# Cross-attention and FP4 feed-forward: part of the first tiles' preparation moved to GpSimd, two small loads packed into another, correlation blocks ordered earlier

## The chip, the cores and the metric

The kernel runs on one core of a Trainium2 chip. The core has five engines that run beside each other, each with its own queue of instructions: TensorE (PE, matrix products), VectorE (DVE), ScalarE (ACT), GpSimd (POOL) and SyncE (SP, which here only issues transfers). The metric is the device time of one execution in microseconds (us); lower is better.

## The reference

Inputs are `x` and a context, both 64 x 128 x 256 in float32. With learned weights the reference computes two residual steps:

```python
# 1. correlation attention; q from layernorm(x), k and v from the context
q  = (layernorm(x) @ Wq + bq).transpose(0, 2, 1)      # 16 channels, length 128
k_ = (ctx @ Wq + bq).transpose(0, 2, 1);  v = the same as k_
corr = real(ifft(fft(q) * conj(fft(k_)))).mean(axis=(0, 1))      # 128 shifts
W, I = top_k(corr, 12);  W = softmax(W)
R3   = sum over the 12 of  W * roll(v, -I)
x = x + (R3 broadcast to 16 heads) @ Wout + bout
# 2. feed-forward with both operands of every product rounded to FP4
def fp4(t):            # blocks of 16 along the last axis
    scale = max|block| / 6
    return nearest of {0, .5, 1, 1.5, 2, 3, 4, 6} * sign * scale
n = layernorm(x)
h = silu(fp4(n) @ fp4(w_gate).T) * (fp4(n) @ fp4(w_up).T)        # 704 wide
x = x + fp4(h) @ fp4(w_down).T
```

The top 12 shifts depend on all of x and all of the context, so the attention term is known only when both have been read. It takes few distinct values: rows that share a residue are given the same 256 numbers, which the kernel keeps in four tiles `O[0]` to `O[3]` (128 x 256, and one more column that gives the mean of each row of O).

## The kernel before, in words

Only the part up to the first feed-forward tiles matters here, and what follows it in order.

**Loads and correlation (0 to about 55 us).** SyncE issues the loads in the order written in `LOADS`. Sixteen blocks `xt` of x, transposed, give the sums that the layernorm and the correlation need. Eight blocks `c0` to `c7` of the context follow (the last in two halves, `c7a`, `c7b`). For each block TensorE forms `pk` = Wq times the block (line L1077), ScalarE adds the bias `Bq` and writes `kT` (L1091), and TensorE adds the correlation of the block to `pg` (L1100, two matmuls a row of blocks). `Wq` (128 x 64 floats) and `Bq` (128 x 1) have loads of their own (L817, L818). Gate and up weights come as `Wg` in three loads (L827). VectorE and ScalarE quantise the weights meanwhile. The quantised weights become `WgL`, `WgH`, `WdH`, `WdL` by transposing transfers (L721); the operand of `WdH` is written by a cast on ScalarE (L754) from `Wdn`, that of `WdL` on VectorE (L761 and L768).

**Attention (55 to about 68 us).** The correlation is copied to `Wcor` (L1150); VectorE finds the top 12 (two rounds of MAX8), softmax weights follow, and `Vn`, `Va`, `Wp` and `O` are formed on TensorE, ScalarE and VectorE (L1459, L1500, L1547, L1584, L1590). ScalarE needs another function table for square roots (a table load, L1549) and later one for Silu (L1621).

**The x stage.** There are 64 tiles of 128 rows. Loads of x bring four tiles at a time (`load_x`, L335): group q holds tiles 4q to 4q+3. `x_parts` (from L425) prepares a group, or a part of it:
- `neg` = minus the new mean of each row (L460, VectorE);
- X += O. On VectorE for the first groups (`add`, L446), for q > 2 by an accumulating transfer that GpSimd issues (L482);
- `cc` = X centred: on VectorE in one instruction together with O for tiles 0 and 1 (L471), else on ScalarE (L498);
- sums of squares on ScalarE (`junk`, L508); absolute maxima per block of 16 on VectorE (`am`, L518); scales and reciprocals (L534 to L561, L572, L578); division by the scale (L585); rounding to the FP4 grid (`k`, L593 to L606, and L338); and `xhl`, the result in two halves of 16 bits (L614);
- `xT`, its transpose: for tiles 0 to 3 by TensorE (L630) with copies out (L636), else by a transposing transfer (L643).

**The feed-forward (`group_ops`, from L1194).** For a tile t: `gu` = gate and up (L1220, TensorE), `g` = silu (L1226, ScalarE), `h` (L1233, VectorE), maxima of h per block (L1243), reciprocals (L1257), division (L1272: GpSimd, but VectorE for tile 0 and the last two), rounding (L1300, L1316 on ScalarE, L338 on VectorE), `hl` (L1325), a transposing transfer, and `pd` = the down product (L1369, L1371). L1388 adds it to X and the result is stored. The reductions of h also read a small strip behind each h that holds the least scale ("least strips", three of them, written on ScalarE at L1601).

**What sets the order.** Every operation is handed to `op(engine, cost, function, r=, w=, dl=, after=...)`. The `Order` class then plans: it keeps a free time for each engine and goes through the ready operations by earliest start and due time (`dl`), with the costs that are written in nanoseconds by hand; `rel` is an earliest time, `after` a mere order, `chain` forces one operation right behind another. The planned order is written out, and each engine's queue is then strictly that order. Waits between engines are semaphores, so an instruction that waits holds up all behind it on its engine. The line that chains a reciprocal to the next tile's h is `if t - 1 in recips`; the line that picks how O is added is `"D" if q > 2 else "V"`.

Of the kernel before, what the change touches and what calls it, by code (L numbers as in the profile page):

```python
# [12 lines left out]
F32 = mybir.dt.float32  # L13
# [6 lines left out]
ALU = mybir.AluOpType  # L20
# [239 lines left out]
@with_exitstack  # L260
def xattn_ffn(ctx: ExitStack, tc: tile.TileContext, x, xt, cx, wq, bq, wo, bo, wgu, wd, out):
    nc = tc.nc
# [87 lines left out]
    RG = (0.0, 0.0, 0.0)  # L350
    TC = 46000.0
    VB = 0
    TF = 49000.0
# [5 lines left out]
    LA = 4000.0  # L359
    BEFORE = 16  # L360
    HOT2 = 70000.0
    ZV, CV, EV = (0, *range(62, 64)), range(61, 64), range(64)
# [10 lines left out]
    FIRST = ((0, 2, "V"),)  # L373
    LOADS = "wg0 x0 wq wg1 x1 wg2 x2 x3 x4 x5 x6 x7 x8 x9 x10 x11 x12 wd x13 x14 x15 bq c0 c1 c2 c3 c4 c5 c6 c7a c7b wo bo"
    TO = 51000.0
# [20 lines left out]
    xT_of = {}  # L396
    adds = {}

    def x_stage(*a, **kw):
        for _ in x_parts(*a, **kw):  # L400
            pass
# [22 lines left out]

    def x_parts(R, q, i0, nt, fast, due, alu, pe_x=False, root=False, both=None, off=0):  # L425
        g, hq = q % 4, q // 4
# [12 lines left out]

        eng = "V"  # L440
        pe = fast
# [24 lines left out]
        for i in tiles:  # L466
            if fast:
                op(
                    "V",
                    336,  # L470
                    lambda i=i: V.scalar_tensor_tensor(  # L471
                        T["cc"].t[:, i], Xq.t[:, i0 + i], T["neg"].t[:, i : i + 1], O[g][:, 0:D], ALU.add, ALU.add
                    ),
                    r=[(Xq, i0 + i), T["neg"], ("O", g)],
                    w=[(T["cc"], i)],
                )
        if alu == "D":
            for i in tiles:
                adds[4 * q + i] = op(
                    "G",  # L480
                    900,
                    lambda i=i: G.dma_start(Xq.t[:, i0 + i], O[g][:, 0:D], accum_op=ALU.add),  # L482
                    r=[("O", g)],
                    w=[(Xq, i0 + i)],
                    lat=LA,
                    port=False,
                )
                adds[4 * q + i].rel = 0.0
        else:
            step = 1 if nt == 1 else 2  # L490
            for lo in range(0, nt, step):
                add(lo, lo + step)
        for i in tiles:
            if not fast:
                op(
                    "A",
                    400,
                    lambda i=i: A.activation(  # L498
                        T["cc"].t[:, i], Xq.t[:, i0 + i], AF.Identity, bias=T["neg"].t[:, i : i + 1]
                    ),  # L500
                    r=[(Xq, i0 + i), T["neg"]],
                    w=[(T["cc"], i)],
                )
# [225 lines left out]
    def d_scales(pool, ring, loaded, dg):  # L729
        s1 = pool.tile([P, 1], F32, name="s1")  # L730
        for h in range(2):
            amax_op(NF, sd[:, h : h + 1], Wdn[:, h : h + 1], NB, ["Wd"], ["sd"])
        op("V", 110, lambda: V.tensor_scalar(sd, sd, 1.0 / 24.0, TINY / 4.0, ALU.mult, ALU.max), w=["sd"])
        op("V", 600, lambda: V.reciprocal(rd, sd), r=["sd"], w=["rd"])
        op("V", 150, lambda: V.tensor_reduce(s1, sd.rearrange("p r b -> p (r b)"), AX.X, ALU.max), r=["sd"], w=["s1"])
        op("V", 130, lambda: V.tensor_scalar(dg[:, 0], ident, s1, None, ALU.mult), r=["s1"], w=["dg"])
        pm_d = ring.new()
        op("PE", 430, lambda: PE.matmul(pm_d.t[:, 0:P], ones, dg[:, 0], start=True, stop=True), r=["dg"], w=[pm_d], dl=18000.0)
        op("V", 200, lambda: V.tensor_reduce(s1, pm_d.t[:, 0:P], AX.X, ALU.max), r=[pm_d], w=["s1"])
        op(  # L740
            "V",
            70,
            lambda: V.tensor_single_scalar(p2[:, 2:3].bitcast(I32), s1.bitcast(I32), 0x7F800000, ALU.bitwise_and),
            r=["s1"],
            w=["p2d"],
        )
# [7 lines left out]
        op("A", 1370, lambda: A.copy(HdN[:, :, 0:NF], Wdn), r=[("Wd", 0), ("Wd", 1)], w=["HD"])  # L754
        S.rel = 0.0

    HdN = XA.bitcast(F16)[:, 0 : 4 * NF].rearrange("p (h n) -> p h n", h=2)
# [28 lines left out]
    with ExitStack() as ph1:  # L786
# [8 lines left out]
        )  # L795
        Wg = wp.tile([P, 11, D], F32, name="Wg")
        Wq = wp.tile([P, 2, 32], F32, name="Wq")
# [18 lines left out]
        loads = {  # L816
            "wq": (180, ["Wq"], lambda: SP.dma_start(Wq, wq)),  # L817
            "bq": (60, ["Bq"], lambda: SP.dma_start(Bq, bq)),  # L818
            "wo": (750, ["Wo"], lambda: SP.dma_start(Wo[:, :, 0:D], wo)),
# [3 lines left out]
        for n, (a0, a1) in enumerate(gch):  # L823
            loads[f"wg{n}"] = (
                340 * (a1 - a0),
                [("Wg", n)],
                lambda a0=a0, a1=a1: SP.dma_start(Wg[:, a0:a1], wgu[:, a0:a1]),  # L827
            )
# [11 lines left out]
        for n in LOADS.split():  # L840
            cost, w, f = loads[n]
            prev = (op("SP", cost, f, w=w, lat=LL, dl=at + DLS, after=prev),)
            at += cost
        Wqc = wp.tile([P, 2, 32], F32, name="Wqc")
        pw = r_q.new()
# [221 lines left out]
        loaded = (load_x(0, dl=TD, after=(wgl,)),)  # L1067
        d_scales(wp, r_q, loaded, dg)
        for j, b0, b1 in [(j, 0, 2) for j in range(7)] + [(7, 0, 1), (7, 1, 2)]:
# [4 lines left out]
            def f_k(ct=ct, pk=pk, b0=b0, b1=b1, n=n):  # L1074
# [12 lines left out]
            op("PE", 30 + 4.2 * n, f_k, r=[(ct, b) for b in range(b0, b1)] + ["Wq"], w=[pk], dl=TK)  # L1087
            op(
                "A",
# [8 lines left out]
            def f_g(bs=range(2 * j + b0, 2 * j + b1)):  # L1098
# [95 lines left out]
    def group_ops(tiles):  # L1194
# [16 lines left out]
        for i, t in enumerate(tiles):  # L1211
# [498 lines left out]
```

## Time and profile before

| | |
|---|---|
| median of 3 runs | 438.52 us (437.1 to 439.69) |
| the profiled execution | 438.42 us, of which 436.5 us are the span |
| first gate/up matmul (tile 0) | 71.64 us |
| gate/up of tile 2, tile 4 | 81.44, 92.67 us |
| busy DVE, ACT, POOL from 70 to 80 us | 9.21, 9.84, 3.85 of 10 |
| PE busy from 200 to 400 us | 199.74 of 200 |
| granted TensorE clock | 0.996 |

Times in lines of the profile are microseconds from the start of the span unless marked ns. A line of a timeline gives start, duration, engine (an engine's name with q is its queue, where transfers are issued), source line, operation, output and inputs by the program's names without buffer numbers, shapes, and how many instructions were taken together. A bracket at its end gives the idle time of that engine just before, and what ended it. In a line of a group the numbers behind the bar are the busy time in all, the mean duration of one in ns, and the idle time in front of them with what ended most of it.

### The profile page before, as it was taken

The page shows a single profiled execution, that of the slowest core. Times are in us where ns is not written, and L with a number is a line of the kernel's source. Part 1 is how long each engine was busy: PE and PEld are TensorE (multiplying, and loading weights), DVE is VectorE, ACT ScalarE, POOL GpSimd, SP SyncE. Part 2 cuts the span into 40 slices and gives each one's busy share as a digit, 9 for nine tenths or more (in the row PEclk, how much of TensorE's full clock was granted, in tenths as well). Part 3 has the DMA queues.
Part 4 walks back from the last instruction along what each step waited for, and adds up shares of the span by engine and source line. Part 5 has one row for each costly group of instructions (what it writes and reads, how often), then busy time and mean ns, then how long its engine had stood idle before and what let it go on. Part 6 is the DMA issues. An engine that isn't in the chain of part 4 may idle for free.

```text
span 436.5 us, 7999 instructions
## 1 busy us (share of the span) xinstructions
PE 418.5 (96%) x2950; PEld 267.5 (61%) x2950; DVE 393.3 (90%) x853; ACT 285.3 (65%) x480; POOL 137.4 (31%) x122
## 2 busy tenths in 40 slices
PE   8999889889898999999999999999999999999996
PEld 8556565446555656566666666666665666566686
DVE  7989589989999999989999989999999999978872
ACT  3887548788596696467946794887579666464410
POOL 1000000444434264344544444454434222324100
PEclk9999999899999999999999999999999999999999
DMA  8999999553797498578757877687678615952362
GB/s 292 414 384 419 322 231 280 124 105 71 152 163 162 106 220 178 137 134 210 158 136 148 212 157 163 139 173 154 117 162 164 156 38 125 188 123 66 96 167 74
DMA packets 152535, 76.61 MB, mean 176 GB/s; under 512 B 134448, under 2 KB 142000, under 8 KB 152496
## 3 DMA queue, kind: packets, MB, share of 16 engines
q1 hardware_dynamic: 145008, 69.29, 60.9%
q0 software_dynamic: 7488, 6.82, 10.9%
q8 instruction: 23, 0.38, 0.4%
q14 instruction: 16, 0.13, 0.1%
HBM read 27.76 MB, written 8.39 MB: 83 GB/s over the span
## 4 chain that ended last, share of the span: by engine, by line
PE 66%; DVE 14%; ACT 9%; DMA 8%; issue 2%; SPq 1%; ACTq 0%
PE gu L1220 38%; PE pd L1369 14%; PE pd L1371 8%; DMA xt<-in_xt_dram 6%; DVE hs L1243 3%; DVE h L1233 2%; DVE hl L1325 2%; DMA ct<-in_cx_dram 2%; ACT junk L508 2%; ACT cc L498 2%; ACT g L1226 1%; DVE am L518 1%; PE pk L1077 1%; DVE hr L1257 1%; DVE cc L585 1%
## 5 line engine op out<-in xcount | busy, mean ns | idle before, releaser
L1220 PE MATMUL gu<-WgH,xT 128*128 128x512 f16 (+1 forms) x768 | 193.1, 363 | 6.0 <-ACT g L1226 2.6
L1220 PEld LDWEIGHTS <-xT 128*128 128x128 f16 x1152 | 112.7, 98 | 116.5 <-issue 6.7
L1272 POOL TENSOR_TENSOR h<-h,hr 128x704 f32<-128x704 f32 x61 | 92.7, 1519 | 195.6 <-DVE hr L1257 168.8
L1220 PE MATMUL gu<-WgL,xT 128*128 128x512 f16 (+1 forms) x384 | 107.9, 363 | 0.0
L1226 ACT ACTIVATE g<-gu,ug 128x704 f32<-128x704 f32 x64 | 53.7, 840 | 43.7 <-PE gu L1220 43.5
L1300 ACT ACTIVATE hk<-h,c_half 128x1408 int16<-128x1408 f32 (+1 forms) x34 | 47.4, 1395 | 37.3 <-POOL h L1272 34.5
L1243 DVE TENSOR_REDUCE hs<-h 128x44 f32<-128x792 f32 x64 | 66.7, 1041 | 2.1
L1233 DVE SCALAR_TENSOR_TENSOR h<-gu,uh,g 128x704 f32<-128x704 f32 x64 | 55.9, 873 | 5.2 <-ACT g L1226 3.4
L482 POOL DMA_DIRECT2D X<-O x36 | 31.9, 983 | 74.3 <-DMA X<-in_x_dram 74.3
L1316 ACT ACTIVATE hc<-hk,c_sub 128x1408 f16<-128x1408 int16 (+1 forms) x32 | 45.6, 1426 | 0.5
L1369 PE MATMUL pd<-WdH,hT 128*128 128x256 f16 x352 | 43.7, 273 | 1.3 <-DMA hT<-hl 1.3
L1369 PEld LDWEIGHTS <-hT 128*128 128x128 f16 x352 | 34.4, 98 | 9.5 <-DMA hT<-hl 1.7
L1325 DVE TENSOR_TENSOR hl<-hc,hsb 128x1408 f16<-128x1408 f16 (+1 forms) x34 | 28.6, 842 | 0.2
L1325 DVE TENSOR_TENSOR hl<-hc,hsl 128x1408 f16<-128x1408 f16 (+1 forms) x34 | 28.5, 840 | 0.0
L1257 DVE RECIPROCAL hr<-hs 128x44 f32<-128x44 f32 x64 | 26.7, 418 | 0.2
L508 ACT ACTIVATE junk<-cc 128x256 bf16<-128x256 f32 x64 | 26.0, 406 | 0.4 <-DVE cc L471 0.2
L1371 PE MATMUL pd<-WdL,hT 128*128 128x256 f16 x192 | 26.2, 273 | 0.0
L1286 ACT ACTIVATE hsb<-hs 128x176 bf16<-128x176 f32 (+1 forms) x34 | 11.4, 335 | 19.8 <-DVE hs L1243 19.8
L498 ACT ACTIVATE cc<-X,neg 128x256 f32<-128x256 f32 x46 | 22.4, 498 | 2.9 <-DVE neg L460 2.9
L929 ACT ACTIVATE xsq<-xt,shift 128x1024 f32<-128x1024 f32 x16 | 17.8, 1145 | 9.5 <-DVE shift L925 6.2
L585 DVE TENSOR_TENSOR cc<-cc,rz 128x256 f32<-128x256 f32 x64 | 23.3, 418 | 0.1
L338 DVE TENSOR_SCALAR hc<-hc 128x1408 int16<-128x1408 int16 (+1 forms) x34 | 16.9, 496 | 5.7 <-ACT hc L1316 5.3
(252 smaller groups left out, 569.4 us busy)
## 6 DMA issues: line engine op xcount, KB each, us to landing
xt<-in_xt_dram SPq DMA_DIRECT2D x16, 512.0 KB, 8.1
ct<-in_cx_dram SPq DMA_DIRECT2D x7, 1024.0 KB, 13.9
X<-in_x_dram SPq DMA_DIRECT2D x12, 512.0 KB, 4.5
out_dram<-X SPq DMA_DIRECT2D x23, 256.0 KB, 2.4
X<-O POOLq DMA_DIRECT2D x36, 128.0 KB, 2.9
XA<-in_x_dram SPq DMA_DIRECT2D x4, 512.0 KB, 5.4
XA<-O POOLq DMA_DIRECT2D x16, 128.0 KB, 2.7
out_dram<-XA SPq DMA_DIRECT2D x7, 256.0 KB, 2.0
```

The source lines that it names most:

```text
L482: lambda i=i: G.dma_start(Xq.t[:, i0 + i], O[g][:, 0:D], accum_op=ALU.add),
L508: lambda i=i: A.activation(T["junk"].t, T["cc"].t[:, i], AF.Square, accum_out=T["ssq"].t[:, off + i : off + i + 1]),
L1220: PE.matmul(pg.t[:, c0:c1], src[:, b], w[:, k, c0:c1], start=(m == 0), stop=(m == 5))
L1226: lambda pg=pg, g=g: A.activation(g.t, pg.t[:, 0:NF], AF.Silu, scale=ug),
L1233: lambda pg=pg, g=g, i=i: V.scalar_tensor_tensor(B["h"].t[:, i, 0:NF], pg.t[:, NF:NG], uh, g.t, ALU.mult, ALU.mult),
L1243: lambda i=i: V.tensor_reduce(B["s"].t[:, i], B["h"].t[:, i].rearrange("p (jj b e) -> p b jj e", b=NB, e=2), AX.XY, ALU.max, apply_absolut ...
L1272: lambda i=i, zv=zv: (V if zv else G).tensor_tensor(per_block(B["h"].t[:, i, 0:NF], NB), per_block(B["h"].t[:, i, 0:NF], NB), spread(B["r" ...
L1300: lambda: A.activation(sub("k"), sub("h")[:, :, 0:NF], AF.Identity, bias=c_half, scale=24.0),
L1316: lambda: A.activation(flat("c"), flat("k"), AF.Identity, bias=c_sub, scale=SUB),
L1325: lambda e=e, part=part: V.tensor_tensor(B["hl"].t[:, 0:nt, e].rearrange("p t (jj n) -> p t jj n", jj=JJ), sub("c").rearrange("p t (jj n) ...
L1369: PE.matmul(pd, hT.t[:, b], WdH[:, :, b], start=(b == 0), stop=False)
L1371: PE.matmul(pd, hT.t[:, b], WdL[:, :, b], start=False, stop=(b == 5))
```

## The change

1. *Loads.* `Wq` and `Bq` lose their own loads. On the host they are put in front of the gate weights, in 66 more columns (64 + 1 + 1 of padding) of the same array; the first weight load brings them, and two small VectorE copies take them out.
2. *Correlation.* The due time of a block's `pg` matmuls was the same for all blocks; now it is earlier by 2.6 us for each block before the last. The cast L754 is placed behind the last `kT` on ScalarE.
3. *Table loads.* The one for square roots is due 12 us earlier and no longer waits for the first O; the one for Silu is due 8 us later.
4. *The x stage.* Tiles 0 and 1: O is added by a GpSimd transfer (`A0 = "D"`), behind the centring that includes it. Tiles 2 and 3: O is added on GpSimd, tile by tile; the centring is the VectorE one with O in it (`C2E = "V"`). Tiles 4 to 7: both the add and the centring run on GpSimd (`A1 = "P"`, `C1 = "G"`). Tiles 8 to 11: the add runs on GpSimd (`Q2A = "P"`). From tile 12 on nothing is different in kind.
5. *Least strips.* They are written on GpSimd, after the first product of the attention that gives O[0].
6. *Feed-forward.* A reciprocal is chained to the next tile's h only from t = 6 on (`CHAIN = 6`).

The planned order comes out of these together. In the changed kernel's written order GpSimd's queue runs: the three strips; the two accumulating transfers of tiles 0 and 1; the add of one of tiles 2 and 3; two accumulating transfers for tiles 12 and 13; four adds and four centrings (tiles 4 to 7); four adds (tiles 8 to 11); two more transfers; the add of the other of tiles 2 and 3; and then transfers between the divisions of h. In VectorE's queue the maxima of tiles 4 to 7 stand, as before, ahead of the end of tiles 2 and 3 and ahead of the first h.

```diff
@@ x_parts
-        eng = "V"
+        eng = "G" if alu in ("P", "PC") else "V"
...
-            if fast:
-                op(
+            if fast or cce == "V":
+                ccs_of[q] = op(
                     "V",
                     336,
...
         for i in tiles:
-            if not fast:
+            if cce == "G":
+                ccs_of[q] = op(
+                    "G",
+                    GC,
+                    lambda i=i: G.tensor_scalar(
+                        T["cc"].t[:, i], Xq.t[:, i0 + i], T["neg"].t[:, i : i + 1], None, ALU.add
+                    ),
+                    r=[(Xq, i0 + i), T["neg"]],
+                    w=[(T["cc"], i)],
+                )
+            elif not fast and cce != "V":
                 op(
                     "A",
                     400,
...
-            "wq": (180, ["Wq"], lambda: SP.dma_start(Wq, wq)),
-            "bq": (60, ["Bq"], lambda: SP.dma_start(Bq, bq)),
...
+        op("V", 100, lambda: V.tensor_copy(Wq.rearrange("p k n -> p (k n)"), Wall[:, 0:64]), r=[("Wg", 0)], w=["Wq"], dl=0.0)
+        op("V", 70, lambda: V.tensor_copy(Bq, Wall[:, 64:65]), r=[("Wg", 0)], w=["Bq"], dl=1000.0)
...
-                dl=TC,
+                dl=TC - CP * (7 - j),
             )
             cool.append(pg_op)
+        hd_op.after.add(k_op)
...
-            if t - 1 in recips:
+            if t - 1 in recips and t >= CHAIN:
...
-    op("A", 1300, lambda: A.activation(warm, c_half, AF.Sqrt), w=["tbl"], dl=TO, after=[*quick, t1_op])
+    op("A", 1300, lambda: A.activation(warm, c_half, AF.Sqrt), w=["tbl"], dl=TO - 12000.0, after=[t1_op])
...
     for t in h_tiles:
         op(
-            "A",
-            350,
-            lambda t=t: A.activation(
-                t[:, :, NF : NF + 2 * NB], ones[:, 0 : 2 * NB].unsqueeze(1).broadcast_to([P, 2, 2 * NB]), AF.Copy, scale=htiny
+            "G",
+            500,
+            lambda t=t: G.tensor_scalar(
+                t[:, :, NF : NF + 2 * NB], ones[:, 0 : 2 * NB].unsqueeze(1).broadcast_to([P, 2, 2 * NB]), htiny, None, ALU.mult
             ),
-            r=[("O", 3)],
             w=["least"],
+            after=first,
+            dl=TG + 12000.0,
         )
...
-        x_stage(R4, 0, i, n, True, TG + i * STEP0, e, True, True)
-    x_stage(R4, 0, 2, 2, False, TG + 2 * STEP0, "V", True, True)
+        x_stage(R4, 0, i, n, True, TG + i * STEP0, A0, True, True)
+    x_stage(R4, 0, 2, 2, F2, TG + DUE2, A2, P2, True, cce=C2E)
...
-        x_stage(R4, 1, i, n, False, TG + DUE1 + d, "V", p, True)
-    op("A", 1300, lambda: A.activation(warm, c_half, AF.Silu), w=["tbl"], dl=TG)
+        x_stage(R4, 1, i, n, False, TG + DUE1 + d, A1, p, True, cce=C1)
+    op("A", 1300, lambda: A.activation(warm, c_half, AF.Silu), w=["tbl"], dl=TG + SILU)
...
-            parts.append((due, x_parts(R4, q, 0, 4, False, due, "D" if q > 2 else "V", both=both, off=4 * n)))
+            parts.append((due, x_parts(R4, q, 0, 4, False, due, "D" if q > DQ else Q2A, both=both, off=4 * n)))
```

The new constants are `CP = 2600.0`, `DQ = 2`, `CHAIN = 6`, `Q2A = "P"`, `A0 = "D"`, `A1 = "P"`, `A2 = "P"`, `C1 = "G"`, `C2E = "V"`, `F2 = False`, `P2 = True`, `DUE2 = 7200.0`, `SILU = 8000.0` and `GC = 450.0`.

More of the change, by code (lines that the diff above doesn't have):

```diff
@@ L260, in xattn_ffn @@
 @with_exitstack
-def xattn_ffn(ctx: ExitStack, tc: tile.TileContext, x, xt, cx, wq, bq, wo, bo, wgu, wd, out):
+def xattn_ffn(ctx: ExitStack, tc: tile.TileContext, x, xt, cx, wo, bo, wgu, wd, out):
     nc = tc.nc
@@ L351, in xattn_ffn @@
     TC = 46000.0
+    CP = 2600.0
     VB = 0
@@ L360, in xattn_ffn @@
     BEFORE = 16
+    DQ = 2
+    CHAIN = 6
+    Q2A = "P"
+    A0 = "D"
+    A1 = "P"
+    A2 = "P"
+    C1 = "G"
+    C2E = "V"
+    F2 = False
+    P2 = True
+    DUE2 = 7200.0
+    SILU = 8000.0
+    GC = 450.0
     HOT2 = 70000.0
@@ L373, in xattn_ffn @@
     FIRST = ((0, 2, "V"),)
-    LOADS = "wg0 x0 wq wg1 x1 wg2 x2 x3 x4 x5 x6 x7 x8 x9 x10 x11 x12 wd x13 x14 x15 bq c0 c1 c2 c3 c4 c5 c6 c7a c7b wo bo"
+    LOADS = "wg0 x0 wg1 x1 wg2 x2 x3 x4 x5 x6 x7 x8 x9 x10 x11 x12 wd x13 x14 x15 c0 c1 c2 c3 c4 c5 c6 c7a c7b wo bo"
     TO = 51000.0
@@ L397, in xattn_ffn @@
     adds = {}
+    ccs_of = {}
     def x_stage(*a, **kw):
@@ L423, in roots, with x_parts @@
         op("V", 75, lambda: V.scalar_tensor_tensor(t, v, TINY / 4.0 / -3.2, y, ALU.mult, ALU.mult), r=[bv, by], w=[bt])
-    def x_parts(R, q, i0, nt, fast, due, alu, pe_x=False, root=False, both=None, off=0):
+    def x_parts(R, q, i0, nt, fast, due, alu, pe_x=False, root=False, both=None, off=0, cce=None):
         g, hq = q % 4, q // 4
@@ L478, in x_parts @@
             for i in tiles:
-                adds[4 * q + i] = op(
+                adds[4 * q + i0 + i] = op(
                     "G",
@@ L487, in x_parts @@
                 )
-                adds[4 * q + i].rel = 0.0
+                adds[4 * q + i0 + i].rel = 0.0
         else:
-            step = 1 if nt == 1 else 2
+            step = 1 if nt == 1 or eng == "G" else 2
             for lo in range(0, nt, step):
@@ L753, in d_scales @@
         G.memset(LdN[:, :, NF : 6 * P], 0.0)
-        op("A", 1370, lambda: A.copy(HdN[:, :, 0:NF], Wdn), r=[("Wd", 0), ("Wd", 1)], w=["HD"])
+        hd_op = op("A", 1370, lambda: A.copy(HdN[:, :, 0:NF], Wdn), r=[("Wd", 0), ("Wd", 1)], w=["HD"])
         S.rel = 0.0
+        return hd_op
     HdN = XA.bitcast(F16)[:, 0 : 4 * NF].rearrange("p (h n) -> p h n", h=2)
@@ L795, in xattn_ffn @@
         )
-        Wg = wp.tile([P, 11, D], F32, name="Wg")
+        Wall = wp.tile([P, 11 * D + 66], F32, name="Wall")
+        Wg = Wall[:, 66:].rearrange("p (a n) -> p a n", a=11)
         Wq = wp.tile([P, 2, 32], F32, name="Wq")
@@ L826, in xattn_ffn @@
                 [("Wg", n)],
-                lambda a0=a0, a1=a1: SP.dma_start(Wg[:, a0:a1], wgu[:, a0:a1]),
+                lambda c0=66 * (n > 0) + a0 * D, c1=66 + a1 * D: SP.dma_start(Wall[:, c0:c1], wgu[:, c0:c1]),
             )
@@ L1067, in xattn_ffn @@
         loaded = (load_x(0, dl=TD, after=(wgl,)),)
-        d_scales(wp, r_q, loaded, dg)
+        hd_op = d_scales(wp, r_q, loaded, dg)
         for j, b0, b1 in [(j, 0, 2) for j in range(7)] + [(7, 0, 1), (7, 1, 2)]:
@@ L1087, in xattn_ffn @@
             op("PE", 30 + 4.2 * n, f_k, r=[(ct, b) for b in range(b0, b1)] + ["Wq"], w=[pk], dl=TK)
-            op(
+            k_op = op(
                 "A",
@@ L1683 @@
     wgu = np.concatenate([wg[_PERM_F], wu[_PERM_F]], 0)[:, _PERM_D]
-    wgu_l = c(wgu.reshape(11, P, D).transpose(1, 0, 2))
+    wgu_l = wgu.reshape(11, P, D).transpose(1, 0, 2).reshape(P, 11 * D)
+    wgu_l = c(np.concatenate([wq_l.reshape(P, 64), bq_l, np.zeros((P, 1), bq.dtype), wgu_l], 1))
     wd_l = c(wd[_PERM_D][:, _PERM_F].reshape(2, P, NF).transpose(1, 0, 2))
@@ L1690 @@
         "cx": cx_l,
-        "wq": wq_l,
-        "bq": bq_l,
         "wo": wo_l,
```

## The prediction

> **What bounds the kernel now.** I read the page's first part, then busy time by stage, then the timelines of single engines around the stage that the change rearranges, then the groups of instructions. TensorE is nearly always busy:
>
> ```profile
> PE 418.5 (96%) x2950; PEld 267.5 (61%) x2950; DVE 393.3 (90%) x853; ACT 285.3 (65%) x480; POOL 137.4 (31%) x122
> ```
>
> That average hides three stages. Until 52.3 us transfers lead: the loads of x and context land one behind another (context blocks every 2.46 us, and the projection of each starts 0.15 to 0.3 us after it). From 55 to about 140 us a chain through VectorE leads. From 140 us on it is TensorE. The busy time by stage shows the last two (columns: length, then PE, PEld, DVE, ACT, POOL busy, granted clock, DMA share, GB/s):
>
> ```profile
> 70.00:80.00 10.00, 9.08 (x56) 4.82 (x55) 9.21 (x28) 9.84 (x29) 3.85 (x5) 1.00 1.04 309
> ...
> 120.00:140.00 20.00, 18.32 (x109) 10.43 (x108) 19.55 (x41) 16.62 (x36) 8.89 (x8) 1.00 0.89 171
> 140.00:200.00 60.00, 58.95 (x382) 37.10 (x381) 56.84 (x118) 38.36 (x62) 23.84 (x21) 1.00 0.71 154
> ```
>
> From 70 to 140 us DVE has hardly a gap, while PE idles. From 140 on PE lacks 1 us in 60. So a delay of the first FFN tiles that VectorE does not make good by 140 us stays in the total. PE's first waits:
>
> ```profile
> 79.51 0.84 PE L630 MATMUL pd<-ident_h,xhl 128*128 128x128 f16 x8 [0.57 <-DVE xhl L614]
> 81.44 1.00 PE L1220 MATMUL gu<-WgH,xT 128*128 128x512 f16 x2 [1.08 <-ACT xT L636]
> ...
> 92.67 0.59 PE L1220 MATMUL gu<-WgH,xT 128*128 128x512 f16 x2 [1.14 <-DVE h L1233]
> ```
>
> The first gate/up matmul (tile 0) starts at 71.64; 81.44 is tile 2, 92.67 tile 4, which waits for VectorE's h of tile 2. VectorE on the way there:
>
> ```profile
> 74.53 1.22 DVE L518 TENSOR_REDUCE am<-cc 128x64 f32<-128x1024 f32 x1
> ...
> 80.56 1.89 DVE L446 TENSOR_TENSOR X<-X,O 128x512 f32<-128x512 f32 x3
> ...
> 90.08 0.34 DVE L338 TENSOR_SCALAR hc<-hc 128x704 int16<-128x704 int16 x1 [1.76 <-ACT hc L1316]
> ...
> 91.67 0.85 DVE L1233 SCALAR_TENSOR_TENSOR h<-gu,uh,g 128x704 f32<-128x704 f32 x1
> ```
>
> The reduction at 74.53 (absolute maxima of tiles 4 to 7) is the place to watch. Behind it in VectorE's queue stand the last steps of tiles 2 and 3 (L338, L578, L614), h of tiles 0 and 1, and the xhl of tiles 4 to 7. Now the two queues that the change ties to it, SyncE's and GpSimd's:
>
> ```profile
> 66.99 1.95 SPq L335 DMA_DIRECT2D X<-in_x_dram  x3
> ...
> 76.14 4.68 POOL L482 DMA_DIRECT2D X<-O  x5 [74.35 <-DMA X<-in_x_dram]
> ```
>
> The first of these three loads (tiles 12 to 15) takes 7.2 us to land, at 74.1. GpSimd, idle for 74 us, starts adding O by DMA at 76.14, 0.75 us after the second load landed (75.39). Five issues take 4.68, 0.94 each.
>
> **The change, part by part.** The sum is made against the profiled execution, 438.42 us (span 436.5 and 1.9 around it), practically the median 438.52.
>
> *Loads.* Two go: Wq (32 KB) and Bq (128 packets of 4 B). Wq landed at 6.11 and the next weights at 8.21, where x loads follow each other by 1.25; Bq lies in the gap from 31.04 (last x) to 34.42 (first context), 3.38 against the usual 2.46. The excess is 0.85 and 0.9. Bq's own landing came 0.83 behind x's, so some is start of a new stream: I take 0.4 and 0.6, together 1.0 (bounds 0, since they overlap others, and 1.75). SyncE's queue loses two issues (0.42, 0.64); the loads behind them wait for the transfers in front, not for their issue. The two new VectorE copies (128x64, 128x1) lie in its idle start; the longest they could cost is 0.5 there, and then the loads would still hide it. The Trainium skill, "DMA: Bandwidth & Descriptors", Anatomy of one DMA, puts about 2 us of fixed cost on each transfer. By that the two would give 4.0; the landings, which overlap, do not allow it.
>
> *End of the correlation.*
>
> ```profile
> 52.56 1.37 ACT L754 CAST XA<-Wdn 128x1408 f16<-128x1408 f32 x1
> ...
> 53.83 0.37 ACT L1091 ACTIVATE kT<-pk,Bq 128x128 f32<-128x128 f32 x1
> ```
>
> The last kT stood behind the cast, though its matmuls were done at 53.28; and all twelve pg matmuls of six blocks (1.60) ran from 53.21 on. With the cast behind it and the earlier blocks done early, the last copy starts 0.5 earlier; I take 0.6 in all (0.4 to 0.9). The cast then ends near 54, and its transposes are issued at 58.97 only.
>
> *Attention.* L761 (0.53) comes in front of the first MAX: +0.2. The Sqrt table load (1.28, then 0.20) moves from between the Va copies to before them: +0.4 for the first. Sum of the prologue: -1.0 -0.6 +0.2 +0.4 = -1.0, and the first gate/up a little more, -1.1, because on VectorE a shorter centring (0.44) takes the place of the add at 65.94 (0.69) ahead of them (bounds -0.3 and -1.9).
>
> *VectorE's adds and centrings.* Six adds L446 (0.63 to 0.69) leave, 3.9; two centrings L471 (0.44) come, 0.9. ScalarE loses six centrings L498 (0.50) and three strips L1601 (0.43); from 80 to 100 us it is busy 14.7 of 20, so this by itself is worth nothing. The strips need 0.2 to 0.5 each on GpSimd, which was idle then; their readers, the reductions of h, come ten us later.
>
> *GpSimd's queue.* This is the step that decides. In the changed order GpSimd runs: strips; two DMA adds (tiles 0, 1); an add (tile 2); **two DMA adds of tiles 12 and 13**; four adds and four centrings of tiles 4 to 7; then tiles 8 to 11 and the rest. The two DMA adds of tiles 12 and 13 wait for the 66.99 load, and tiles 4 to 7, whose data landed at 64.31, are queued behind this wait. The reduction that was at 74.53 now waits for the last of these centrings. Its time:
> - the load lands at 74.1 - 1.0, plus what the two new DMA adds for tiles 0 and 1 (around 64, 256 KB) take from the transfers. At the 309 GB/s of 70 to 80 us that is 0.8, read and write counted 1.7, or 0: so 73.1 to 74.8, taken 74.0;
> - wake-up 0.75 (low: 0.15, as the context's readers): 74.75;
> - two DMA issues at 0.94: 76.6 (low: 1.1, by the 0.54 between their starts);
> - four two-input adds of 128x256, from the only such group on GpSimd:
>
> ```profile
> L1272 POOL TENSOR_TENSOR h<-h,hr 128x704 f32<-128x704 f32 x61 | 92.7, 1519 | 195.6 <-DVE hr L1257 168.8
> ```
>
>   scaled by 256/704: 0.55 each, 2.2: 78.8 (low 1.9);
> - four one-input centrings, no row: between the 128x256 IOTA (0.34) and the add (0.55); 0.45 taken, 1.8: last centring at 80.6 (all low 77.6, all high 82.2).
>
> The Trainium skill, "GPSIMD Engine Reference", 3.1, has one-input loops at 1.03 to 1.8 cycles an element, an estimate of 0.22 to 0.38 us each, which would end them 0.3 to 0.9 earlier. The same section says "use DVE for elementwise" stays the rule, which speaks against the move; the runs will show it.
>
> VectorE would be free for the reduction at 74.5 - 1.1 - 1.4 (two adds of tiles 4 to 7) - 0.7 (tiles 2, 3) + 0.9 = 72.2. It starts at 80.6 + 0.2 = 80.8: idle of 8.6 us, and 6.3 later than before. ScalarE waits too, with squares of these tiles standing ahead of tile 2's quantisation and the Silu table load.
>
> *What then catches up.* By h of tile 2: the three adds at 80.56 are gone (-1.9), and the idle of 1.76 at 90.08 mostly closes, since ScalarE now works beside a later VectorE (-1.7). So h of tile 2 comes at 91.67 + 2.7 = 94.4, and tile 4's matmuls follow. From there VectorE has the same work, 0.2 to 0.3 less, up to 140 us. Result: 438.4 + 2.7 - 0.3 = 440.8. All savings (1.1 in front, 3.0 of VectorE's work) are already inside; they pay about half of the wait. Unchaining tiles 1 to 5 lets a reciprocal be split from h: no work, between 0 and one 0.42 either way.
>
> **Rivals.**
> 1. *The lag is absorbed.* After tile 4 PE still idles at 110.80 (1.28), 115.97 (0.59), 130.56 (1.58), 174.22 (0.97): 4.4 us. If half of this closes because VectorE's later queue is shifted less than PE, the end is 440.8 - 2.2 = 438.6. For it: some of these end on a transfer. Against: those transfers follow VectorE's xhl and hl.
> 2. *Not slower: GpSimd is done early.* Same place, one quantity, the last centring. It decides at 80.6 - 2.4 = 78.2: before that the total falls below 438.4. With the low ends (77.6) it is 437.8; with the load landing 2 us sooner, as would follow if the whole transfer queue drains faster, 435.8. The floor, no wait at all, is 438.4 - 1.1 - 3.0 = 434.3. For it: wide bounds on wake-up and centring. Against: the load is the eighth in a full queue.
> 3. *Worse.* The DMA adds of tiles 0 and 1 collide with the transposes and X loads (DMA share 1.06 there), GpSimd's adds run slower beside VectorE: last centring at 82.2 or later, 442.4 to 443.5.
> 4. *Loads hidden anyway:* the prologue gives nothing, and all shifts by 1.0: 441.8. It lies within the forecast's own range.
>
> **How the numbers follow.** Forecast (439.5 to 442) 0.42; rival 1 0.20; rival 2 0.25; rivals 3 and 4 0.13. About 0.5% (2.2 us) can be told from no change. Under 436.3 lies most of rival 2's lower part and a mixture with 1: 0.25. Over 440.7: more than half of the forecast's case, and 3 and 4: 0.46. Between: 0.29. The range 435.0 to 443.5 leaves out one in ten at each end.
>
> **What would show it.** Right: GpSimd idle before its DMA adds until about 75, VectorE idle 7 to 9 us in front of a reduction at about 81, released by GpSimd's centring; tile 2's first gate/up at 84 to 86, tile 4's near 95; first gate/up near 70.5; PE busy without gaps from 140 on. Wrong: a centring that ends before 78, or tile 4 earlier than 92.7; the first gate/up not before 71.6 would refute the loads' part. A much faster result needs tiles 4 to 7 to be centred before VectorE asks for them.

## The result, and the profile after

The changed kernel takes 447.59 us (median; 446.97 to 447.93), the kernel before 438.52: a ratio of 1.0231, 95% interval 1.0201 to 1.0261. The forecast was 440.8 with a range up to 443.5. The direction was right, the size was not: +9.1 us instead of +2.3. The profiled execution took 447.93 us, with a span of 445.9.

The first part of its page, with the granted clock from the second part:

```profile
PE 419.5 (94%) x2944; PEld 267.6 (60%) x2944; DVE 395.0 (89%) x851; ACT 283.3 (64%) x471; POOL 152.7 (34%) x141
...
PEclk9999999579899999999999999999999999999999
```

The busy times hardly moved, GpSimd's excepted (137.4 to 152.7); PE's share fell because the span grew. The two lowest digits of the clock, 5 and 7, cover 78 to 100 us. Busy time by stage (columns: length, then PE, PEld, DVE, ACT, POOL busy, granted clock, DMA share, GB/s):

```profile
70.00:80.00 10.00, 7.30 (x36) 3.44 (x36) 2.14 (x10) 1.57 (x6) 6.69 (x10) 1.00 0.94 300
80.00:90.00 10.00, 2.18 (x11) 1.19 (x12) 8.48 (x15) 7.75 (x17) 7.46 (x10) 0.51 0.28 41
90.00:100.00 10.00, 10.00 (x44) 5.06 (x43) 8.59 (x16) 7.48 (x19) 2.33 (x2) 0.81 0.42 93
120.00:140.00 20.00, 20.00 (x125) 12.26 (x124) 19.59 (x46) 17.36 (x35) 7.93 (x7) 0.97 0.62 137
140.00:200.00 60.00, 58.11 (x377) 36.53 (x376) 57.73 (x122) 38.89 (x63) 25.74 (x22) 1.00 0.77 157
```

VectorE, 9.21 of 10 us busy from 70 to 80 before, now has 2.14, and GpSimd has 6.69. The hole in PE follows from 80 to 90. GpSimd's timeline (start, length, engine, line, operation, count, idle time before and its releaser):

```profile
73.31 1.77 POOL L497 DMA_DIRECT2D X<-O  x2 [7.25 <-DMA X<-in_x_dram]
74.45 3.40 POOL L461 TENSOR_TENSOR X<-X,O 128x256 f32<-128x256 f32 x4
77.20 4.21 POOL L513 TENSOR_SCALAR cc<-X,neg 128x256 f32<-128x256 f32 x4
80.80 3.32 POOL L461 TENSOR_TENSOR X<-X,O 128x256 f32<-128x256 f32 x4
```

This is the queue that the prediction drew: a wait for the load of tiles 12 to 15, two DMA issues, four adds, four centrings, and the reduction on VectorE behind the last of them. VectorE's timeline goes on:

```profile
81.45 1.22 DVE L543 TENSOR_REDUCE am<-cc 128x64 f32<-128x1024 f32 x1 [9.30 <-POOL cc L513]
82.58 1.70 DVE L338 TENSOR_SCALAR k<-k 128x512 int16<-128x512 int16 x1
...
103.72 0.46 DVE L1353 TENSOR_TENSOR hl<-hc,hsb 128x704 f16<-128x704 f16 x1
104.10 1.85 DVE L1353 TENSOR_TENSOR hl<-hc,hsl 128x704 f16<-128x704 f16 x1
```

The first line was predicted (80.8, idle of 8.6). The second and the last are what the prediction lacked. The form of L338 at 82.58 takes 0.29 elsewhere in this trace, and here 1.70. The two L1353 have the same shape, one after the other: 0.46 and 1.85. The first long one begins while GpSimd does the four adds from 80.80 to 84.12 and ends 0.16 us after the last of them. The second begins while GpSimd does the division of h below, and ends 0.39 us after it:

```profile
103.89 1.67 POOL L1300 TENSOR_TENSOR h<-h,hr 128x704 f32<-128x704 f32 x1
```

PE, in the same stretch, waits twice:

```profile
84.81 1.16 PE L655 MATMUL pd<-ident_h,xhl 128*128 128x128 f16 x8 [7.16 <-DVE xhl L639]
...
88.97 1.01 PE L1248 MATMUL gu<-WgH,xT 128*128 128x512 f16 x2 [3.00 <-DVE h L1261]
```

**An account of the loss.** Follow VectorE from the moment that O of tile 0 is written to the end of xhl of tiles 8 to 11; the first gate/up matmul of tile 8, behind those, starts some 4 us later. I split that time into idle time, *stretch* (what an instruction took beyond the usual duration of its line and shape in the same trace, summed), and ordinary work. What one takes as the usual duration moves the stretch of a run by half a us or so; the rest of the account follows from the trace alone.

| us | before | after | difference |
|---|---|---|---|
| O of tile 0 starts | 63.51 | 61.76 | -1.75 |
| VectorE idle | 3.23 | 11.45 | +8.22 |
| VectorE stretched | 0.19 | 5.25 | +5.06 |
| ordinary work | 45.80 | 42.91 | -2.89 |
| xhl of tiles 8 to 11 done | 112.72 | 121.38 | +8.66 |
| gate/up of tile 8 | 116.56 | 125.52 | +8.96 |
| last matmul ends | 433.21 | 442.38 | +9.17 |

The lag at 121 us is the lag at the end. The prediction had the first, second and fourth rows within 1.5 us. It had no third row. Of that row about half (2.7) lies in instructions beside GpSimd's adds (L610 at 65.33, L338 at 82.58, L576 at 85.02) and half (2.7) beside divisions of h (L338 at 102.46 and 111.30, L1353 at 104.10). The experiments ask whether that reading of the trace holds.

### The profile page after: what moved, and what is told of

The parts are those of the page before. It is cut to its first block, busy times and chain, and to the rows that moved or that the text cites. A ratio compares the mean times of both kernels' runs of the same rounds, so it can differ in the third digit from the quotient of the medians.

```text
span 445.9 us, 7993 instructions
## 1 busy us (share of the span) xinstructions
PE 419.5 (94%) x2944; PEld 267.6 (60%) x2944; DVE 395.0 (89%) x851; ACT 283.3 (64%) x471; POOL 152.7 (34%) x141
## 4 chain that ended last, share of the span: by engine, by line
PE 73%; DMA 10%; DVE 7%; ACT 4%; POOL 2%; issue 2%; SPq 1%; ACTq 0%; POOLq 0%
PE gu L1248 45%; PE pd L1397 16%; PE pd L1399 9%; DMA xt<-in_xt_dram 5%; DMA ct<-in_cx_dram 2%; DMA X<-in_x_dram 1%; ACT g L1254 1%; DVE hl L1353 1%; DVE h L1261 1%; PE pk L1104 1%; POOL X L461 1%; ACT hk L1328 1%; DVE cc L610 1%; DMA xT<-xhl 1%; POOL cc L513 1%
## 5 line engine op out<-in xcount | busy, mean ns | idle before, releaser
L1248 PE MATMUL gu<-WgH,xT 128*128 128x512 f16 (+1 forms) x768 | 195.2, 365 | 10.3 <-DVE h L1261 5.7
L497 POOL DMA_DIRECT2D X<-O x38 | 35.1, 968 | 10.4 <-DMA X<-in_x_dram 7.2
L1353 DVE TENSOR_TENSOR hl<-hc,hsl 128x1408 f16<-128x1408 f16 (+1 forms) x34 | 29.9, 879 | 0.0
L1353 DVE TENSOR_TENSOR hl<-hc,hsb 128x1408 f16<-128x1408 f16 (+1 forms) x34 | 28.5, 839 | 0.2
L543 DVE TENSOR_REDUCE am<-cc 128x64 f32<-128x1024 f32 (+1 forms) x17 | 19.6, 1152 | 9.4 <-POOL cc L513 9.3
L624 ACT ACTIVATE k<-cc,c_half 128x1024 int16<-128x1024 f32 (+1 forms) x16 | 17.9, 1118 | 14.9 <-DVE cc L610 14.9
L338 DVE TENSOR_SCALAR hc<-hc 128x1408 int16<-128x1408 int16 (+1 forms) x34 | 18.4, 541 | 6.3 <-ACT hc L1344 6.2
L610 DVE TENSOR_TENSOR cc<-cc,rz 128x256 f32<-128x256 f32 x64 | 23.9, 427 | 0.1
```

The costliest lines, as they stand in the source:

```text
L610: (G if alu == "G" else V).tensor_tensor(per_block(T["cc"].t[:, i], XB), per_block(T["cc"].t[:, i], XB), spread(T["rz"].t[:, i], XB), ALU. ...
L1248: PE.matmul(pg.t[:, c0:c1], src[:, b], w[:, k, c0:c1], start=(m == 0), stop=(m == 5))
L1353: lambda e=e, part=part: V.tensor_tensor(B["hl"].t[:, 0:nt, e].rearrange("p t (jj n) -> p t jj n", jj=JJ), sub("c").rearrange("p t (jj n) ...
```

## The experiments

Theories: **W**, the wait of the reduction behind GpSimd's queue; **S**, VectorE's instructions are held while GpSimd computes; **C**, the lower TensorE clock after the hole; **D**, the dropped chaining of h's reciprocals (`CHAIN = 6` lets the tiles below 6 run without it). The expectations were written before the letters were settled: in them theory A is W, and theory D is S, with the chaining as one of its cases. All ratios are to the kernel before, with 95% intervals.

**e1_order: tiles 4 to 7 go ahead of the DMA adds of tiles 12 and up.**

```diff
+    for t in adds:
+        if t >= 12:
+            adds[t].after.add(ccs_of[1])
     heat_buf(Q["pd"].new(), HOT2)
```

> The changed kernel, but the accumulating transfers of tiles 12 and up stand behind the four centrings of tiles 4 to 7 in GpSimd's queue; same instructions. Theory A (the wait for the load of tiles 12 to 15 in that queue costs the time): GpSimd's adds start when O[1] is there, about 68.1; with the steps of the changed kernel's own profile (0.69 an add, 0.9 to 1.0 a centring) and one add of tile 8 between, the last centring ends near 75.6, the reduction of tiles 4 to 7 starts near 75.8 instead of 81.45, VectorE's idle falls from 9.3 to 3 or 4 us, and the total falls by 5.5 to 8, to 439.5 to 442. Rival B (GpSimd is too slow for this work wherever it stands, or its adds slow VectorE down): idle above 6 us, total above 445.

Measured: 442.84 us, 1.0096 [1.0062, 1.0130], so 4.75 us of 9.1 come back (1.35% of 2.31% by the ratios, which compare each run with the kernel before of its own session). The total is just above the range of theory A. GpSimd, then VectorE:

```profile
68.08 4.12 POOL L461 TENSOR_TENSOR X<-X,O 128x256 f32<-128x256 f32 x5 [2.02 <-ACT O L1612]
72.57 3.69 POOL L513 TENSOR_SCALAR cc<-X,neg 128x256 f32<-128x256 f32 x4 [0.37 <-DVE neg L475]
```

```profile
76.30 1.22 DVE L543 TENSOR_REDUCE am<-cc 128x64 f32<-128x1024 f32 x1 [2.26 <-POOL cc L513]
```

The reduction comes 5.15 us sooner, and the idle time in the account falls from 11.45 to 4.88. The stretch rises from 5.25 to 7.38, since VectorE now works while GpSimd does tiles 4 to 11. W is half of the loss or a little more, and the time is still above the kernel before.

**e2_q1_back, e7_q2_vec, e8_q12_chain: GpSimd's arithmetic is taken back step by step.** e2 gives tiles 4 to 7 back to VectorE and ScalarE, e7 tiles 8 to 11 as well, e8 restores the chaining too.

```diff
-    A1 = "P"
+    A1 = "V"
-    C1 = "G"
+    C1 = None
...
-    Q2A = "P"
+    Q2A = "V"
...
-    CHAIN = 6
+    CHAIN = 0
```

> The changed kernel with tiles 4 to 7 prepared as before: O added on VectorE, centred on ScalarE. All else stays, the transfers for tiles 12 and 13 with their wait too, but nothing of VectorE's next work stands behind them. A: VectorE's idle before the reduction is under 1 us, the total 435.5 to 438 (prologue 1.3 us earlier than before, no adds for tiles 8 to 11 on VectorE). B' (the loss lies in other parts: transfers for tiles 0 and 1, unchained reciprocals, table loads): above 442.

> The run with tiles 4 to 7 prepared as before, and now the adds of tiles 8 to 11 on VectorE again too. CHAIN = 6 stays, and so do the additions on GpSimd for tiles 2 and 3. Theory D: at 74.8 to 79.8 three VectorE instructions were stretched from 0.93 to 3.99 us together while GpSimd added; without these adds that goes, two adds of 0.69 come to VectorE. Net 1.7 us less: 441.5 to 443. Rival (GpSimd's adds relieve VectorE): 444.5 to 446.

> As the last, and CHAIN = 0: of the x stage only tiles 0 to 3 remain changed (transfers for 0 and 1, GpSimd adds for 2 and 3, VectorE's centring for 2 and 3), with the strips, table loads, packed loads and correlation order of the change. Theories A and D together: no wait on GpSimd's queue in VectorE's, one stretched instruction (0.6 us at 65.3); total 436.5 to 439, as the kernel before. Rival (one of these remaining parts costs several us too): above 440.

Measured: e2 444.11, 1.0123 [1.0091, 1.0155], a miss of 6 us (the rival B' held); e7 440.52, 1.0075 [1.0052, 1.0097], 1 us below its range; e8 437.08, 1.0001 [0.9975, 1.0027]. In e2 the long wait is gone (idle 4.60), and yet it is slower than before: the stretch is 7.60. GpSimd, then VectorE beside it, in e2:

```profile
75.42 3.74 POOL L461 TENSOR_TENSOR X<-X,O 128x256 f32<-128x256 f32 x4
```

```profile
76.66 1.92 DVE L603 TENSOR_TENSOR slo<-am,shb 128x64 f16<-128x64 f32 x1
78.50 1.30 DVE L639 TENSOR_TENSOR xhl<-k,shb 128x512 f16<-128x512 f16 x1
```

The same two in e7, where GpSimd does not add these tiles:

```profile
76.09 0.37 DVE L603 TENSOR_TENSOR slo<-am,shb 128x64 f16<-128x64 f32 x1
76.39 0.41 DVE L639 TENSOR_TENSOR xhl<-k,shb 128x512 f16<-128x512 f16 x1
```

1.92 becomes 0.37, 1.30 becomes 0.41, although VectorE now adds O to four tiles more. That is S. Of what e7 still has stretched (4.77), 3.7 stands beside divisions of h:

```profile
92.76 1.51 POOL L1300 TENSOR_TENSOR h<-h,hr 128x704 f32<-128x704 f32 x1 [1.97 <-DVE hr L1285]
```

```profile
92.78 1.52 DVE L426 TENSOR_SCALAR y<-ssq 128x4 int32<-128x4 int32 x1
```

A 128x4 instruction (0.16 as a rule) lasts as long as GpSimd's. In the kernel before the chaining keeps this apart: beside the divisions of its trace run 61 instructions of h, 58 reductions of h and one other, none longer than usual by more than about 0.10. e8 restores it: stretch 1.04, time that of the kernel before. How much of this step is the stretch isn't shown: VectorE's idle time rises from 1.15 to 3.33, so xhl of tiles 8 to 11 is done only 0.6 us sooner (112.21 against 112.81). On PE three tiles of down products stand ahead of the gate/up of tile 8 in e7, four in e8, and that gate/up starts at 117.02 and 117.10; a tile of down products takes 1.85.

Undone in this order the parts are worth 1.1% (tiles 4 to 7), 0.5% (tiles 8 to 11) and 0.7% (chaining), that is about 4.7, 2.1 and 3.3 us, each with an uncertainty of 1 to 2. All others together are left with 0.0%, which can be gains and costs that cancel (f3 below has gains).

**e6_chain and e10_order_chain: the chaining alone, in the changed kernel and in e1.**

```diff
-    CHAIN = 6
+    CHAIN = 0
```

> The changed kernel with the reciprocal, the next h and its reduction chained for all tiles again (CHAIN = 0), nothing else. Theory D (while GpSimd runs a division of h, VectorE's short and fast-mode instructions last until it ends; the chain kept h and its reduction beside the division, and without it others land there: L338 at 102.46 took 0.93 for 0.35, L1353 at 104.10 took 1.85 for 0.52, L338 at 111.30 took 1.27 for 0.52): these stretches, 2.7 us, go, and with them part of the 2.5 us in which TensorE waited at 114; total 444.5 to 446.5. Rival: the order of the reciprocals is worth nothing next to the wait at 72 to 81: 447 to 448.

> The run with GpSimd's queue reordered (442.84), and CHAIN = 0. Theory D: the stretches at 98 to 107 us (2.4 us in three instructions) go, as in the step from 440.52 to 437.08: 439.5 to 441.5. Rival (as with the chain alone restored in the changed kernel, 448.4: VectorE's later xhl of tiles 8 to 11 then holds up tile 8): 442.5 to 444.

Measured: e6 448.40, 1.0251 [1.0210, 1.0292]; e10 443.36, 1.0145 [1.0109, 1.0181]. Both miss what theory D expected: no gain from what is worth 3.3 in e8. In e10 VectorE did gain: the stretch falls from 7.38 to 4.91, and xhl of tiles 8 to 11 is done at 113.81 instead of 116.69. But PE's timeline shows

```profile
118.43 1.04 PE L1248 MATMUL gu<-WgH,xT 128*128 128x512 f16 x2 [7.31 <-DMA xT<-xhl]
```

The restored chaining also changes the planned order on PE: only two tiles of down products stand ahead of the gate/up of tile 8, four in the kernel before, the changed one and e8. PE runs dry. The gate/up of tile 8 starts 2.4 earlier than in e1 (118.43 against 120.84), but two tiles of down products, 1.85 each, that e1 has behind it by then are still to do, and the last matmul ends at 438.43 (438.10). e6 has the same two tiles, and an idle time of 6.55 in the same place. So what the chaining is worth depends on this order, and 3.3 us is the price of the step from e7 to e8 only.

**e5_warm: 30 idle products in PE's queue keep the clock up** (their result is never read).

```diff
+    for _ in range(30 if q == 0 and i0 == 2 and i == 0 else 0):
+        PE.matmul(pt.t[:, 0:P], ident, ident, start=True, stop=True)
```

> The changed kernel with 30 idle products of 128x128 in TensorE's queue between gate/up of tile 1 and the transposes of tile 2, some 6.6 us of work where it waited 7.2; the output is the same. Theory C (part of the loss is that TensorE's granted clock falls to a half while it waits, 0.50 from 84 to 92 us): gate/up of tiles 2 and 3, 10.3 us in the changed kernel, takes 8 to 9 us, and the total falls by 1 to 2.5, to 445 to 446.5. Rival: VectorE sets the pace there whatever the clock: 447.2 to 448.

Measured: 447.69, 1.0215 [1.0174, 1.0255], against 447.59 for the changed kernel: the rival's range. The granted clock from 80 to 84 us (the figure before the last two), in the changed kernel and in e5:

```profile
80.00:84.00 4.00, 0.00 (x0) 0.00 (x0) 2.55 (x2) 3.94 (x13) 4.00 (x7) 0.52 0.00 0
```

```profile
80.00:84.00 4.00, 4.00 (x38) 4.00 (x37) 2.59 (x2) 3.94 (x13) 4.00 (x7) 1.00 0.00 0
```

The gate/up of tile 2 still starts at 88.94 (88.97), released by VectorE's h. In e5 the clock is higher from 88 to 96 us too (0.62 and 0.95, against 0.50 and 0.77). C is out: the low clock of an engine that waits for another cost nothing here.

**f1_dose: e3 (below) plus 24 GpSimd adds of 128x128 that nobody reads.** The rest of the queues is e3's.

```diff
+    for _ in range(24):
+        op("G", 10, lambda: G.tensor_tensor(dose, O[0][:, 0:P], O[0][:, 0:P], ALU.add), r=[("O", 0)], w=["dose"], after=first, port=False, dl=TG)
```

> The run with only the loads and correlation order changed, with 24 extra GpSimd additions of 128x128 into a tile that nothing reads, from the moment O[0] is written (about 62 us); the queues of the other engines are the same instruction for instruction, and nobody waits for the additions. Theory D (VectorE's instructions with two SBUF inputs or in a fast mode stand still while GpSimd computes): of some 0.4 us each they last to about 72 us, and 10 or more VectorE instructions there stretch by 0.2 to 0.5 each; reductions, reciprocals and instructions with an input in PSUM keep their times; total up by 2 to 5, to 439.5 to 442.5. Rival (only waits in queues cost): 437 to 438.

Measured: 437.61, 1.0006 [0.9983, 1.0028], e3 being at 0.9983. The total lies in the rival's range, so theory D missed the size. The adds ran from 62.05 to 75.9, and VectorE beside them was stretched, but by little: 1.99 in the account against 0.19, e.g. L611 with 0.96 where e3 has 0.76. Of that, 1.25 was taken out of VectorE's idle time (3.97 to 2.72). The GpSimd adds came 0.58 apart here, which may be why a held instruction soon got through; those of the changed kernel came 0.69 apart and the divisions took 1.52. This run says that the mere presence of GpSimd work is no constant tax; it does not fix a law of its size.

**f4_q2_dma: the changed kernel with the adds of tiles 8 to 11 by DMA.**

```diff
-    Q2A = "P"
+    Q2A = "D"
```

> The changed kernel with O added to tiles 8 to 11 by transfers instead of GpSimd's adder; the wait for tiles 12 and 13 in GpSimd's queue stays. Theory D: L338 at 82.58, which lasted 1.70 beside these adds, falls to 0.3, and L576 behind it from 0.74 to 0.2: total down by 1.4 to 2, to 445.5 to 446.3. Rival: VectorE's later work absorbs it: 447 to 448.

Measured: 447.88, 1.0234 [1.0188, 1.0280]. L338 beside those adds fell back from 1.70 to 0.28, but others were caught now: at 83.43 L639 takes 0.96 (usually 0.42). The stretch falls by about 0.4 and the idle time rises by 0.4; nothing reaches the end, as the rival said. This L639 began 0.84 us before GpSimd's next add, beside six DMA issues. The same instruction does it in e1, beside DMA issues alone:

```profile
78.72 0.95 DVE L639 TENSOR_TENSOR xhl<-k,slo 128x512 f16<-128x512 f16 x1
```

So issues by GpSimd aren't always free for VectorE either.

**e3_loads_only: no GpSimd part at all,** only the packed loads, the earlier correlation blocks and the cast behind them; the rest is as before, the table loads and the strips too (their lines are left out of the cut below).

```diff
-    CHAIN = 6
-    Q2A = "P"
-    A0 = "D"
-    A1 = "P"
-    A2 = "P"
...
+    CHAIN = 0
+    Q2A = "V"
+    A0 = "V"
+    A1 = "V"
+    A2 = "V"
...
-    SILU = 8000.0
+    SILU = 0.0
...
```

> The kernel before with the packed weights, the earlier correlation blocks and the cast behind the last kT; x stage, strips, table loads and reciprocals as before. The changed kernel's first gate/up came at 70.35 against 71.64. A: the gain in front reaches the end, since VectorE's chain and then TensorE carry it: 437.0 to 437.8 (-0.7 to -1.5). Rival: the gain is swallowed by the idle that TensorE has anyway between 78 and 131 us: 438.2 to 438.8.

Measured: 437.39, 0.9983 [0.9956, 1.0009]: inside the range of A, but the interval takes in no change. In the trace PE ends 1.61 earlier (431.60). Together a small gain is likely, not shown.

**e12_dma_adds and f3_best: looking for a better kernel.** e12 is e3 with the adds of tiles 0, 1 and 8 to 11 by DMA; f3 loads ScalarE's table for the square root ahead of the copies of Va in addition.

```diff
-    A0 = "V"
-    Q2A = "V"
+    A0 = "D"
+    Q2A = "D"
...
-    op("A", 1300, lambda: A.activation(warm, c_half, AF.Sqrt), w=["tbl"], dl=TO, after=[*quick, t1_op])
+    op("A", 1300, lambda: A.activation(warm, c_half, AF.Sqrt), w=["tbl"], dl=TO - 12000.0, after=[t1_op])
```

> The run with only the loads and the correlation order changed, and in addition O added to tiles 0 and 1 and to tiles 8 to 11 by accumulating transfers that GpSimd issues (three VectorE adds fewer, 1.9 us at 80 to 82), all else as before. If transfers relieve VectorE without stretching it (the five issued from 76.1 to 80.8 in the kernel before stretched nothing), VectorE's chain to tile 4 shortens by up to 1.9 us: 435 to 437 with the gain in front. Rival: the transfers wait for their loads, and those of tiles 12 and up come later, or ScalarE sets the pace by then: 437 to 438.5.

> The run with loads, correlation order and transfers for tiles 0, 1 and 8 to 11, and in addition the early table load for square roots; no arithmetic on GpSimd beyond what the kernel before has. In the changed kernel and the runs with that load early the first gate/up came at 70.1 to 70.6, in the runs without it at 72.5. If VectorE's chain then runs earlier by as much up to the xhl of tiles 8 to 11: 435 to 436.5, better than both kernels. Rival: the first tiles are earlier, but the chain to tile 8 is as long as before: 437 to 438.

Measured: e12 437.36, 0.9993 [0.9971, 1.0015], in the rival's range; VectorE's work falls by 1.5 against e3, its idle time grows by 1.2. f3 434.09, 0.9931 [0.9900, 0.9963]: it beats both kernels, the kernel before by 0.7%. The table load, at 60.43 between the copies in e12, stands at 58.87 ahead of them, in a wait for PE:

```profile
60.43 1.28 ACT L1577 ACT_TABLE_LOAD   x1
```

```profile
58.87 1.28 ACT L1577 ACT_TABLE_LOAD   x1
```

The first gate/up starts at 69.54 (72.48 in e12), and xhl of tiles 8 to 11 is done at 108.45 (111.08). In the changed kernel this gain is hidden behind the wait. GpSimd issues transfers here, and computes nothing until the divisions:

```profile
PE 416.6 (96%) x2946; PEld 266.0 (61%) x2946; DVE 391.1 (90%) x852; ACT 285.2 (66%) x480; POOL 142.9 (33%) x128
...
PEclk9999999999999999999999999999999999999999
```

## Why the prediction was wrong

**Right, by its steps.** *Loads and correlation:* the last context block landed 2.0 earlier (52.32 to 50.30), predicted 1.0 with bounds of 0 and 1.75. The 2 us a transfer that the prediction quotes stand in a section on transfers issued by GpSimd; these two were SyncE's. The first gate/up came 1.29 earlier (71.64 to 70.35), predicted 1.1, and here luck has a part. e3 has the same loads and correlation but the late table load: O of tile 0 starts at 61.55, yet the first gate/up at 72.47, later than before. The early table load, priced at +0.4, is what brings it forward (f3 against e12: by 2.9). *GpSimd's queue:* the load landed at 72.77 (74.0), the first DMA add started 0.54 later (0.75), the adds followed at a pitch of 0.69 (0.55) and the centrings at 0.90 (0.45, bounds 0.34 and 0.55). The last was mis-sized, by 1.8 over the four; the earlier load and quicker issues (1.14 for 1.88) paid for most of it, and the last centring ended at 81.4 (80.6; the high end that the prediction gives, 82.2, adds up to 81.8). VectorE idled 9.30 in one piece (8.6), the reduction started at 81.45 (80.8). *VectorE's work* fell by 2.89 (about 3.0). *The wait of 1.76* did close, as predicted: up to h of tile 2 VectorE idles 6.9 us more than before, and 8.6 less 1.7 is 6.9.

**Wrong: "What then catches up".** The step that fails is "From there VectorE has the same work, 0.2 to 0.3 less, up to 140 us", and the sum for h of tile 2 before it. They are true of the list of instructions and false of their time: from 61 to 121 us VectorE's instructions were stretched by 5.06 us more, because some stood beside a GpSimd add or division and lasted until it ended. About 2.7 of it comes ahead of h of tile 2, which was predicted at 94.4, a lag of 2.7, and was written at 96.64, a lag of 5.0; tile 4's matmuls came at 99.14. The rest comes behind it, with two waits for ScalarE (0.88 and 0.66), and the lag grows to 9. This term is missing in the sum, and its absence from the range is why the range missed too. Rival 3 had "GpSimd's adds run slower beside VectorE"; the trace shows VectorE slower beside GpSimd. The trace of before could have warned only indirectly: beside divisions it has hardly anything but reductions and h. The kernel's source says more. Its planner has a rule, switched off (`self.lock` is False), by which operations of VectorE and GpSimd wait for each other's end, unless they are marked `port=False`; among the marked ones are the reductions, the reciprocals, h and GpSimd's DMA adds.

*Unchaining, "no work, between 0 and one 0.42 either way",* is the second mis-sized term: about 2.7 us of the changed kernel's stretch stands beside divisions, and the step from e7 to e8 is 3.3 us, in which PE's order moved too. It costs no work, but it puts other instructions beside the divisions.

**The page that spoke of it.** The Trainium skill, "GPSIMD Engine Reference", Specifications, says that GpSimd shares its SBUF interfaces with VectorE, with contention when a VectorE instruction runs in its two-port mode or has two SBUF inputs. The prediction did not weigh it; it read the rule on choice of engine in the same page as one on GpSimd's own speed. This case's runs agree in part: the instructions held are those on SBUF data (0.16 to 1.52, 0.37 to 1.92, 0.52 to 1.85), and h, which has an operand in PSUM, the reductions and the reciprocals are not.

**The rivals.** 1 (lag absorbed): no; PE lacks 1.89 in 60 us after 140, and the lag of 8.96 at tile 8 is 9.17 at the end. 2 (GpSimd early): no; its last centring would have had to end by 78.2. e1 shows that even 76.3 is not enough: the stretch is still there. 3 (worse) had the right direction, for another reason: its 82.2 was not reached (81.4). 4 (loads hidden): the landing was earlier, but e3, which changes only the loads and the correlation, ends within the noise of the kernel before, so it isn't excluded.

**What stays open.** W and S share the loss as 8.2 and 5.1 in the account, against 2.9 and 1.8 saved. e1 and the series e2, e7, e8 support both, but no single run took away S alone in the changed kernel: e6, the nearest, fell into PE's order, and f4 moved the stretch elsewhere. How the 3.3 us of the chaining divide between VectorE and PE's order is open too. That the long instructions are *held* by the shared interface, rather than slowed by something else that GpSimd does, is read from their ends and from the cited page; no run isolates it.

## What to carry to other kernels

Before work goes to an idle engine, look up what waits in front of it in that engine's in-order queue, then ask which instructions of the bound engine will run *beside* it: here a free GpSimd cost 5 us of VectorE's time without adding one instruction to it. Where a trace shows an odd but constant pairing (only reductions and h beside divisions), take it as something that keeps the time down, and price its removal. And a part whose removal gives nothing back may have changed the planned order elsewhere; read that engine's next wait before dropping the theory.

## What the runs showed of the hardware

- A VectorE instruction on SBUF data that began beside GpSimd arithmetic could last until the GpSimd instruction ended, or up to 0.4 us longer, however small it was: 128x4 in 1.52 us instead of 0.16. Next to several GpSimd adds in a row it could miss the gap between them: 128x64 in 1.92 instead of 0.37. Reductions, reciprocals and instructions with an operand in PSUM kept their time within about 0.10. Not every instruction on SBUF data was held: both L639 of e7 at 76.39 and 76.72 took 0.41 beside an add (spans on GpSimd are rough, above all behind DMA issues).
- DMA issues by GpSimd held nothing in the trace of before (about 120 VectorE instructions beside issues alone, none longer by more than 0.10). In e1 and f4 one L639 each took 0.95 for 0.42 beside several issues in a row.
- GpSimd's one-input centring, with a scalar per partition, was slower than its two-input add of the same 128x256: pitch 0.90 against 0.69.
- The granted clock fell to about 0.5 in PE's hole, and still was 0.81 on average from 90 to 100 us; that cost nothing here, as e5 shows.
